# Row sums of layer 0 on column tiles, and VectorE of layer 0 in program order

## The chip, the cores and the metric

The kernel runs on one core of a Trainium2 chip. A core has a matrix engine (TensorE, "PE" in the profile, its weight loads "PEld"), VectorE ("DVE"), ScalarE ("ACT"), GpSimd ("POOL") and the sync engine ("SP"), which here issues most DMA transfers. They run side by side and wait for each other by semaphores. SBUF is the working memory of 128 partitions, PSUM the small memory in eight banks that TensorE writes. The metric is the device time of one execution in microseconds (us): the median of several runs.

## The reference, cut to what matters

Two layers on an input of 4 images of 128 channels and 64x64 pixels, all in float32. Layer 0 is attention over the 4096 pixels of each image; layer 1 (a cumulative attention and a feed-forward part with choice of experts) follows on 128-channel tokens. The change touches layer 0.

```python
def _L0_conv_ref(x, w1, b1, a1, w2, b2, a2, wa, ba, aa):
    N, C, H, W = x.shape
    HW = H * W
    e1 = _conv1x1(x, w1, b1, a1).reshape(N, -1, HW)
    e2 = _conv1x1(x, w2, b2, a2).reshape(N, -1, HW)
    asm = _conv1x1(x, wa, ba, aa).reshape(N, C, HW)
    score = jnp.einsum('nci,ncj->nij', e1, e2)
    score = jax.nn.softmax(score, axis=2)
    out = jnp.einsum('nij,ncj->nci', score, asm)
    return out.reshape(N, C, H, W)
...
x = x + _L0_conv_ref(_gn(x), L0_conv_w1, ...)
t = _to_tokens(x)
```

`_conv1x1` is a matrix product over channels, a bias and a PReLU; e1 and e2 have 64 channels, asm 128; `_gn` normalizes groups of 4 channels over the whole image.

## The kernel before

**Tiling.** For each image `b` (4) and each block `qb` of 512 queries (8) the kernel walks over 4096 keys in 16 steps `p` of two chunks of 128 keys; an image and a block, so 16 steps, is called a spot here, numbered 0 to 31. `probs` (L1978) makes scores `sc` by four matmuls, two chunks on the lower and the upper 64 rows of the array at the same time, takes `Exp` on ScalarE into `pr` (three buffers) and adds `pr` into `acc` on VectorE, with a copy in its place at p = 0. `weigh` (L1998) multiplies `pr` with the values `am`: two accumulating `av` banks, "o" for the lower and "t" for the upper 64 keys of a chunk. A float32 matmul is two records in the profile. The scores are made two steps ahead of `weigh`, by a list `queue`.

**The end of a spot** is the code under `if p == NPR - 1` in the step loop. After the last `weigh`, and the scores of the next spot's second step:

- `collect` (L2012) copies the lower half to `o` on ScalarE, adds the upper on VectorE, and folds the two halves of `acc` into `sums`.
- `row_sums` (L2030), for the spot before (`done`), sums `sums` over its 128 partitions: four matmuls with 128 columns of `sums` as weights and a column of ones moving, into `pd` (bank tag "sm"), which is copied to `rows` and inverted to `inv`.
- For a block `k` of the next image, `project` (L1928) makes queries and keys: `pe` on TensorE, ScalarE's bias into `y`, VectorE's PReLU by `z` into `e1` and `e2`, with two transfers on SP's queue (one by way of `side`); `value` (L1953) makes values: `pa` (tag "sm"), `ya`, `za`, `am`. `normal` (L1921) makes the input `xn` of the block after.
- `finish` (L2044) transposes `o` of the spot before on TensorE into `otr` (tag "x"), and VectorE multiplies by `inv` and adds the input `xr`, into `t`. `fetch` (L2023) loads the next `xr`.

Spot 0 also makes blocks 2 to 7 of image 0, on even steps. Images 1 to 3 are prepared during the image before: their statistics (`stat`, `chain`) in its first spot (image 1: spot 1), then one block at the end of each spot, two at the end of spot 1. In image 3 the ends of spots hold layer 1's first work in place of the next image: `normals`, `tokens`, `keys` (`f_pk`, silu, product, reduction), and, at `point()`, pieces of a scan that are due (`later(n, ...)` puts a piece off by n points). `LAG` blocks on, layer 1 goes on alone.

**Order.** TensorE's order is that of the program text. For the other engines a scheduler in the framework orders the instructions when the program is built, by its own estimates, and pools of buffers (one bank for each of the tags "x", "sm", "o", "t", two of "kv") add waits. `tc.manual_schedule(engines=...)` takes an engine out of that and keeps program order.

## Time and profile before

| | us |
|---|---|
| median of 3 runs | 2310.56 (2310.31 to 2311.3) |
| the profiled execution | 2303.66, span 2301.8 |
| mean granted TensorE clock | 0.995 |
| from the first `av` (25.50) to the last spot's `pd` (1529.82) | 1504.32 |
| one step in a spot, 8 `av` and 4 `sc` records | 2.57 |
| end of a spot with one projection beyond its step (22 of them) | 3.59 |
| end of spot 1, two projections | 7.14 |
| ends of spots 25 to 29 (layer 1's keys in them); of spot 30 | 10.39 to 10.40; 11.37 |

The profiled execution is one run among others; a sum of durations is held against its own time. In a timeline a row is start, length, engine, line, operation, tile written <- tiles read, shape, and in brackets the engine's idle time before and what ended it. A row with xN is N records in a run, and its length reaches from the first start to the last end, so neighbouring rows overlap in the pipeline. The granted clock is full except in a few stretches of 3.41 us or 6.83 us at half.

### The profile page before, as it was taken

The page shows a single profiled execution, that of the slowest core. Times are in us where ns is not written, and L with a number is a line of the kernel's source. Part 1 is how long each engine was busy: PE and PEld are TensorE (multiplying, and loading weights), DVE is VectorE, ACT ScalarE, POOL GpSimd, SP SyncE. Part 2 cuts the span into 40 slices and gives each one's busy share as a digit, 9 for nine tenths or more (in the row PEclk, how much of TensorE's full clock was granted, in tenths as well). Part 3 has the DMA queues.
Part 4 walks back from the last instruction along what each step waited for, and adds up shares of the span by engine and source line. Part 5 has one row for each costly group of instructions (what it writes and reads, how often), then busy time and mean ns, then how long its engine had stood idle before and what let it go on. Part 6 is the DMA issues. An engine that isn't in the chain of part 4 may idle for free.

```text
span 2301.8 us, 43187 instructions
## 1 busy us (share of the span) xinstructions
PE 2238.5 (97%) x18352; PEld 1163.8 (51%) x18352; DVE 1447.1 (63%) x2380; ACT 1092.2 (47%) x1328; POOL 174.4 (8%) x380
## 2 busy tenths in 40 slices
PE   7999999999999999999999999999999999999997
PEld 3644444444444444444444444456556555566663
DVE  7666565655666565556555666667867777875643
ACT  2343334433333443344445554445566676565751
POOL 0000000000000000000000000011121121222311
PEclk9999999999999999999999999999999999999999
DMA  2000010000010000001000000020211211213488
GB/s 76 33 12 16 10 45 9 17 9 9 11 52 9 9 12 13 9 9 44 9 5 5 5 5 10 5 50 26 66 44 40 65 52 41 59 55 116 138 322 302
DMA packets 78555, 104.77 MB, mean 46 GB/s; under 512 B 8976, under 2 KB 44816, under 8 KB 78352
## 3 DMA queue, kind: packets, MB, share of 16 engines
q1 hardware_dynamic: 77264, 99.81, 13.9%
q8 instruction: 146, 2.39, 0.4%
q0 software_dynamic: 512, 1.05, 0.2%
q10 hardware_dynamic: 576, 1.05, 0.1%
q14 instruction: 57, 0.47, 0.1%
HBM read 78.55 MB, written 17.04 MB: 42 GB/s over the span
## 4 chain that ended last, share of the span: by engine, by line
PE 87%; DVE 6%; ACT 3%; DMA 2%; issue 1%; SPq 0%; POOL 0%; ACTq 0%; DVEq 0%; POOLq 0%
PE av L2009 37%; PE sc L1984 18%; PE f_pv L1128 9%; PE f_pk L973 8%; PE f_pt L1151 3%; PE f_po L1174 2%; PE pd L2035 1%; PE f_po L1186 1%; ACT f_e1a L980 1%; PE pa L1957 1%; DMA x<-in_x_dram 1%; PE pe L1931 1%; DVE f_e1a L981 1%; DVE f_e1a L982 1%; PE f_pl L1294 1%
## 5 line engine op out<-in xcount | busy, mean ns | idle before, releaser
L2009 PE MATMUL av<-pr,am 64*128 64x512 f32 x4096 | 977.7, 592 | 2.4 <-ACT pr L1989 2.4
L1989 ACT ACTIVATE pr<-sc 128x1024 f32<-128x1024 f32 x512 | 524.1, 1024 | 781.2 <-PE sc L1984 766.9
L1996 DVE TENSOR_TENSOR acc<-acc,pr 128x1024 f32<-128x1024 f32 x480 | 586.6, 1222 | 484.8 <-ACT pr L1989 480.5
L2009 PEld LDWEIGHTS av<-pr,am 64*128 64x128 f32 x4096 | 401.8, 187 | 472.9 <-issue 458.1
L1984 PE MATMUL sc<-e,e 64*128 64x512 f32 x2048 | 534.9, 591 | 3.3 <-DMA e<-side 3.3
L1984 PEld LDWEIGHTS sc<-e,e 64*128 64x128 f32 x2048 | 201.5, 187 | 234.7 <-issue 229.2
L1128 PE MATMUL f_pv<-f_held,f_ama 128*32 128x256 f32 x4096 | 237.5, 381 | 6.1 <-ACT f_e1a L980 5.1
L973 PE MATMUL f_pk<-f_held,f_ama 128*128 128x512 f32 x512 | 234.9, 603 | 0.0
L1133 ACT ACTIVATE f_amb<-f_pv 128x1024 f32<-128x1024 f32 x128 | 131.1, 1025 | 130.1 <-PE f_pv L1128 129.4
L981 DVE TENSOR_TENSOR f_e1a<-f_e1a,f_held 128x1024 f32<-128x1024 f32 x128 | 156.9, 1226 | 48.6 <-ACT f_e1a L980 48.3
L980 ACT ACTIVATE f_e1a<-f_pk 128x1024 f32<-128x1024 f32 x128 | 129.8, 1025 | 110.3 <-PE f_pk L973 56.1
L1128 PEld LDWEIGHTS f_pv<-f_held,f_ama 128*32 128x32 f32 x4096 | 129.2, 110 | 100.7 <-ACT f_e1a L980 11.9
L982 DVE TENSOR_REDUCE f_e1a<-f_e1a 128x8 f32<-128x1024 f32 x128 | 155.2, 1217 | 3.5
L973 PEld LDWEIGHTS f_pk<-f_held,f_ama 128*128 128x128 f32 x512 | 92.5, 190 | 108.3 <-issue 101.1
L1092 POOL COPY f_held<-f_e1a 32x32 f32<-32x32 f32 x128 | 30.7, 240 | 909.8 <-DVE f_e1a L1074 564.1
L1151 PE MATMUL f_pt<-f_amb,f_held 128*32 128x128 f32 x1920 | 83.2, 276 | 0.8 <-ACT f_amb L1133 0.8
L918 POOL MEMSET f_held<- 128x1024 f32 x1 | 1.0, 957 | 1036.6 <-DVE xn L1922 1036.6
L1151 PEld LDWEIGHTS f_pt<-f_amb,f_held 128*32 128x32 f32 x1920 | 60.0, 109 | 10.4 <-issue 5.2
L1192 DVE TENSOR_TENSOR t<-t,f_po 128x512 f32<-128x512 f32 (+1 forms) x33 | 22.1, 671 | 56.0 <-PE f_po L1186 56.0
L956 ACT ACTIVATE f_xl<-t,ln_nb,ln_rs 128x128 f32<-128x128 f32 x128 | 52.8, 491 | 0.8 <-PE pa L1957 0.8
L1275 ACT ACTIVATE f_x<-t,f_gnb,f_grs 128x128 f32<-128x128 f32 x122 | 49.7, 482 | 0.4 <-DVE f_gnb L1254 0.4
L1993 DVE COPY acc<-pr 128x1024 f32<-128x1024 f32 x32 | 22.2, 694 | 39.3 <-ACT pr L1989 39.3
(300 smaller groups left out, 1797.8 us busy)
## 6 DMA issues: line engine op xcount, KB each, us to landing
f_e2a<-f_rd SPq DMA_DIRECT2D x128, 128.0 KB, 2.9
xr<-in_xtok_dram SPq DMA_DIRECT2D x32, 256.0 KB, 3.0
f_table<-f_x SPq DMA_DIRECT2D x62, 128.0 KB, 2.0
out_dram<-t SPq DMA_DIRECT2D x14, 512.0 KB, 3.8
x<-in_x_dram SPq DMA_DIRECT2D x12, 512.0 KB, 6.4
e<-e SPq DMA_DIRECT2D x32, 128.0 KB, 2.2
f_ama<-f_rd SPq DMA_DIRECT2D x16, 256.0 KB, 3.8
f_e1b<-f_rd SPq DMA_DIRECT2D x16, 256.0 KB, 6.0
```

The costliest lines, as they stand in the source:

```text
L956: nc.scalar.activation(xl[:, c, :], t[:, b * NCH + i, :], AF.Identity, bias=ln_nb[:, b, i : i + 1], scale=ln_rs[:, b, i : i + 1],)
L973: nc.tensor.matmul(pk[:, i, :], xt_at(n)[:, bass.ts(c, P)], env.wks[:, bass.ts(i, BLK)], start=True, stop=True,)
L980: nc.scalar.activation(flat, pk.rearrange("p i x -> p (i x)"), AF.Silu)
L981: nc.vector.tensor_mul(ks, ks, env.qb)
L982: nc.vector.tensor_reduce(s[:, (n % GB) * CPB + c, :], ks, AX.X, ALU.add)
L1128: nc.tensor.matmul(pv[a * CH : (a + 1) * CH, i, :], xt_at(m)[:, bass.ts(c * NA + i, CH)], env.wvs[:, bass.ts(a, HH * C)], start=True, stop ...
L1133: nc.scalar.activation(env.amb[:, bass.ts(c, HD)], pv.rearrange("p i x -> p (i x)"), AF.Silu)
L1151: nc.tensor.matmul(env.pt[i * CH : (i + 1) * CH, :], lhs, rhs, start=i not in env.begun, stop=False, skip_group_check=True,)
L1984: nc.tensor.matmul(sc[:, u, :], e2[halves[u], p, :], e1[halves[u], cols], start=True, stop=True,)
L1989: nc.scalar.activation(pr, sc, AF.Exp)
L1996: nc.vector.tensor_add(acc, acc, pr)
L2009: nc.tensor.matmul(av, am[h, j, :], pr[h, u, :], start=(j == 0), stop=(j == NCH - 1))
```

## The change

Five parts, all in layer 0:

- **Row sums.** `row_sums` now has a 128x32 block of ones as weights and 128 columns of `sums` moving, four times, each on 32 columns of the array (so each quarter of the rows of `pd` holds 128 sums, repeated 32 times). VectorE copies the result back into `sums`, `row_turn` transposes it on TensorE into a bank of tag "t" (that of the upper `av`), and `row_divide` copies every 32nd column to `rows` and inverts.
- **Order.** VectorE keeps program order in all of layer 0. `project` and `value` are cut in five parts (`project`, `value`, `queries`, `others`, `values`), `finish` in `turn_output` and `finish`; the end of a spot is written out in that order, with `row_turn` after the first block's `value` and `row_divide` after its `queries`. The fold into `sums` becomes `fold`, at the end of it all.
- **Adding up.** `add_up` does the sum of step p after `weigh` of step p (it was with the scores, two steps ahead); at p = 0 nothing is copied, at p = 1 the first two `pr` are added.
- **Image 1's load and statistics** come later: the load at step 13 of spot 0, `stat` one step later, `normal(0)` at step 14.
- **Image 3.** The first `keys` of an end comes between `row_sums` and `row_turn`; `otr` has the tag "sm"; at the end of layer 0 `row_sums` of the last spot comes at once, with `keys(LAG, 1)` ahead of `row_turn`, and `last_turn` at the next point.

```diff
@@ -1881,6 +1881,7 @@
                 make_block_diagonal(nc, gavg, C // 32)
                 nc.vector.tensor_scalar_mul(gavg, gavg, 32.0 / C)
 
+                l0.enter_context(tc.manual_schedule(engines={mybir.EngineType.DVE}))
                 made = {}
 
                 def preparation(b):
...
@@ -1926,11 +1927,15 @@
                         xn_of[k] = xn
 
                     def project(k):
-                        cols = bass.ts(k, BLK)
                         pe = ps.tile([P, BLK], F32, tag="x", name=f"pe_{b}_{k}")
                         nc.tensor.matmul(pe, w12, xn_of[k], start=True, stop=True)
                         y = tmp.tile([P, BLK], F32, tag="y", name=f"y_{b}_{k}")
                         nc.scalar.activation(y, pe, AF.Identity, bias=b12)
+                        y_of[k] = [y]
+
+                    def queries(k):
+                        (y,) = y_of[k]
+                        cols = bass.ts(k, BLK)
...
                         nc.sync.dma_start(out=e1[R:, cols], in_=e1[:R, cols])
+                        y_of[k] = (y, z)
+
+                    def others(k):
+                        y, z = y_of.pop(k)
...
@@ -1957,9 +1966,12 @@
                             nc.tensor.matmul(
                                 pa[:, c, :], xn[:, bass.ts(c, P)], was, start=True, stop=True
                             )
+                        pa_of[k] = pa
+
+                    def values(k):
                         y = tmp.tile([P, CPB, C], F32, tag="y", name=f"ya_{b}_{k}")
                         nc.vector.tensor_tensor(
-                            y, pa, bas.unsqueeze(1).to_broadcast([P, CPB, C]), ALU.add
+                            y, pa_of.pop(k), bas.unsqueeze(1).to_broadcast([P, CPB, C]), ALU.add
                         )
                         z = tmp.tile([P, CPB, C], F32, tag="z", name=f"za_{b}_{k}", bufs=1)
                         nc.vector.tensor_scalar(
@@ -1970,7 +1982,14 @@
                             op0=ALU.max, op1=ALU.add,
                         )
 
-                    return stat, (chain0, chain1, chain2), normal, project, value
+                    def make(k):
+                        project(k)
+                        value(k)
+                        queries(k)
+                        others(k)
+                        values(k)
+
+                    return stat, (chain0, chain1, chain2), normal, (project, value, queries, others, values), make
 
                 NPR = NCH // 2
                 steps = [(b, qb, p) for b in range(B) for qb in range(NBLK) for p in range(NPR)]
@@ -1987,14 +2006,18 @@
                         )
                     pr = tmp.tile([P, 2, BLK], F32, tag="pr", name=f"pr_{b}_{qb}_{p}", bufs=3)
                     nc.scalar.activation(pr, sc, AF.Exp)
+                    return pr
+
+                def add_up(b, qb, p, pr):
                     if p == 0:
+                        acc_of[b, qb] = pr
+                    elif p == 1:
                         acc = small.tile([P, 2, BLK], F32, tag="acc", name=f"acc_{b}_{qb}")
+                        nc.vector.tensor_add(acc, acc_of[b, qb], pr)
                         acc_of[b, qb] = acc
-                        nc.vector.tensor_copy(acc, pr)
                     else:
                         acc = acc_of[b, qb]
                         nc.vector.tensor_add(acc, acc, pr)
-                    return pr
 
                 def weigh(b, qb, p, pr):
                     am = made[b][2]
@@ -2015,10 +2038,13 @@
                     o = tmp.tile([P, BLK], F32, tag="o", name=f"o_{b}_{qb}")
                     nc.scalar.copy(o, lower)
                     nc.vector.tensor_add(o, o, upper_)
+                    o_of[b, qb] = (o,)
+
+                def fold(b, qb):
                     acc = acc_of.pop((b, qb))
                     sums = tmp.tile([P, BLK], F32, tag="sums", name=f"sums_{b}_{qb}", bufs=1)
                     nc.vector.tensor_add(sums, acc[:, 0, :], acc[:, 1, :])
-                    o_of[b, qb] = (o, sums)
+                    o_of[b, qb] += (sums,)
 
                 def fetch(b, qb):
                     xr = tmp.tile([P, CPB, C], F32, tag="xr", name=f"xr_{b}_{qb}", bufs=1)
@@ -2029,63 +2055,89 @@
                     pd = ps.tile([P, BLK], F32, tag="sm", name=f"pd_{b}_{qb}")
                     for c in range(CPB):
+                        rows_ = slice(c * (P // CPB), (c + 1) * (P // CPB))
                         nc.tensor.matmul(
-                            pd[:, c : c + 1], sums[:, bass.ts(c, P)], ones, start=True, stop=True
-                        )
-                    nc.vector.tensor_copy(rows[:, at], pd[:, :CPB])
+                            pd[rows_, :P], ones.to_broadcast([P, P // CPB]), sums[:, bass.ts(c, P)],
+                            start=True, stop=True,
+                        )
+                    nc.vector.tensor_copy(sums[:, :P], pd[:, :P])
+
+                def row_turn(b, qb):
+                    o, sums, xr = o_of[b, qb]
+                    pd = ps.tile([P, BLK], F32, tag="t", name=f"pdt_{b}_{qb}")
+                    nc.tensor.transpose(pd[:, :P], sums[:, :P], ident)
+                    o_of[b, qb] += (pd,)
+
+                def row_divide(b, qb):
+                    o, sums, xr, pd = o_of[b, qb]
+                    at = bass.ts(b * NBLK + qb, CPB)
+                    nc.vector.tensor_copy(rows[:, at], pd[:, : P : P // CPB])
                     inv = tmp.tile([P, CPB], F32, tag="inv", name=f"inv_{b}_{qb}")
                     nc.vector.reciprocal(inv, rows[:, at])
                     o_of[b, qb] = (o, inv, xr)
 
-                def finish(b, qb):
-                    o, inv, xr = o_of.pop((b, qb))
-                    ptr = ps.tile([P, CPB, C], F32, tag="x", name=f"otr_{b}_{qb}")
+                def turn_output(b, qb):
+                    o, inv, xr = o_of[b, qb]
+                    tag = "x" if b + 1 < B else "sm"
+                    ptr = ps.tile([P, CPB, C], F32, tag=tag, name=f"otr_{b}_{qb}")
                     for c in range(CPB):
                         nc.tensor.transpose(ptr[:, c, :], o[:, bass.ts(c, P)], ident)
+                    o_of[b, qb] = (ptr, inv, xr)
+
+                def finish(b, qb):
+                    ptr, inv, xr = o_of.pop((b, qb))
...
-                stat, chain, normal, project, value = preparation(0)
+                stat, chain, normal, parts, make = preparation(0)
                 for k in range(NBLK):
                     stat(k)
                 for f in chain:
                     f()
                 for k in range(2):
                     normal(k)
-                    project(k)
-                    value(k)
+                project, value, queries, others, values = parts
+                project(0)
+                value(0)
+                project(1)
+                for k in range(2):
+                    queries(k)
+                    others(k)
+                    values(k)
+                    if k == 0:
+                        value(1)
+                normal(2)
                 queue = [probs(*steps[0]), probs(*steps[1])]
                 done, todo = None, []
                 env.xl_pool = lambda name: tmp.tile([P, CPB, C], F32, tag="xn", name=name)
                 for n, (b, qb, p) in enumerate(steps):
-                    weigh(b, qb, p, queue.pop(0))
+                    pr = queue.pop(0)
+                    weigh(b, qb, p, pr)
+                    add_up(b, qb, p, pr)
                     if (b, qb) == (0, 0) and p % 2 == 0 and p // 2 + 2 < NBLK:
                         k = p // 2 + 2
-                        normal(k)
-                        project(k)
-                        value(k)
-                        if k == NBLK - 1:
-                            xs_of[1] = load_x(1)
+                        make(k)
+                        if k + 1 < NBLK:
+                            normal(k + 1)
                     if b + 1 < B:
                         first = 1 if b == 0 else 0
                         if qb == first:
                             if p == 0:
                                 prep[b + 1] = preparation(b + 1)
                                 todo = list(range(NBLK))
-                            stat, chain, normal, project, value = prep[b + 1]
-                            if 1 <= p <= NBLK:
-                                stat(p - 1)
-                            elif p == NBLK + 1:
-                                chain[0]()
+                            stat, chain, normal, parts, make = prep[b + 1]
+                            if 2 <= p <= NBLK + 1:
+                                stat(p - 2)
+                                if p == NBLK + 1:
+                                    chain[0]()
                             elif p in (11, 13):
                                 chain[(p - 9) // 2]()
-                            elif p == 15:
+                            elif p == 14:
                                 normal(0)
                     if b > 0 and 2 <= qb < 6 and p % 2 == 0:
                         tile_stats(tmp, b - 1, (qb - 2) * NBLK + p // 2)
@@ -2093,46 +2145,77 @@
                         close_stats(b - 1)
                     if b == B - 1 and qb > 0 and p % 4 == 3 and p < NPR - 1:
                         point()
+                    if p == NPR - 1:
+                        collect(b, qb)
                     if n + 2 < len(steps):
                         queue.append(probs(*steps[n + 2]))
+                    if n == NPR - 3:
+                        xs_of[1] = load_x(1)
                     if p == NPR - 1:
-                        collect(b, qb)
                         if done:
                             row_sums(*done)
                         mine = []
                         if todo:
                             left = NBLK - qb
                             mine = [todo.pop(0) for _ in range(-(-len(todo) // left))]
+                        fresh = done and b < B - 1
                         for k in mine:
-                            _, _, normal, project, value = prep[b + 1]
+                            _, _, normal, (project, value, queries, others, values), _ = prep[b + 1]
                             project(k)
                             value(k)
+                            if fresh:
+                                row_turn(*done)
+                                queries(k)
+                                row_divide(*done)
+                            else:
+                                queries(k)
+                            others(k)
+                            values(k)
                             if k + 1 < NBLK:
                                 normal(k + 1)
                             elif b + 2 < B:
                                 xs_of[b + 2] = load_x(b + 2)
                             else:
                                 env.hold_weights()
+                            fresh = False
                         if b == B - 1:
                             if qb == 0:
                                 env.first_rooms()
+                            else:
+                                keys(min(qb, LAG + 1) - 1, 0)
+                            row_turn(*done)
+                            row_divide(*done)
+                            if qb == 0:
                                 normals(0)
                                 tokens(0)
                             elif qb <= LAG:
-                                for c in range(CPB):
+                                for c in range(1, CPB):
                                     keys(qb - 1, c)
                                 tokens(qb)
+                            turn_output(*done)
                             if qb < LAG:
                                 normals(qb + 1)
                             point()
+                        elif fresh:
+                            row_turn(*done)
+                            row_divide(*done)
+                        if done and b < B - 1:
+                            turn_output(*done)
                         if done:
                             finish(*done)
+                        fold(b, qb)
                         fetch(b, qb)
                         done = (b, qb)
-                later(1, lambda: row_sums(*done))
-                later(1, lambda: finish(*done))
-                keys(LAG, 0)
+
+                def last_turn():
+                    turn_output(*done)
+                    finish(*done)
+
+                later(1, last_turn)
+                row_sums(*done)
                 keys(LAG, 1)
+                row_turn(*done)
+                row_divide(*done)
                 point()
 
         def last_root():
```

More of the change, by code (lines that the diff above doesn't have):

```diff
@@ L1895, in preparation @@
                     made[b] = (e1, e2, am)
-                    xn_of = {}
+                    xn_of, y_of, pa_of = {}, {}, {}
                     def stat(k):
@@ L2031, in row_sums @@
                     o, sums, xr = o_of[b, qb]
-                    at = bass.ts(b * NBLK + qb, CPB)
                     pd = ps.tile([P, BLK], F32, tag="sm", name=f"pd_{b}_{qb}")
                     for c in range(CPB):
+                        rows_ = slice(c * (P // CPB), (c + 1) * (P // CPB))
                         nc.tensor.matmul(
-                            pd[:, c : c + 1], sums[:, bass.ts(c, P)], ones, start=True, stop=True
-                        )
-                    nc.vector.tensor_copy(rows[:, at], pd[:, :CPB])
+                            pd[rows_, :P], ones.to_broadcast([P, P // CPB]), sums[:, bass.ts(c, P)],
+                            start=True, stop=True,
+                        )
+                    nc.vector.tensor_copy(sums[:, :P], pd[:, :P])
[8 more added lines that the diff above has]
+                    nc.vector.tensor_copy(rows[:, at], pd[:, : P : P // CPB])
                     inv = tmp.tile([P, CPB], F32, tag="inv", name=f"inv_{b}_{qb}")
```

## The prediction

> **What bounds the kernel now.** I read the page's busy times and slices first, then the chain of waits, then the timeline around single ends of spots. A spot is one block of 512 queries of one image: 16 steps of `probs` and `weigh`, 32 spots in layer 0.
>
> ```profile
> PE 2238.5 (97%) x18352; PEld 1163.8 (51%) x18352; DVE 1447.1 (63%) x2380; ACT 1092.2 (47%) x1328; POOL 174.4 (8%) x380
> PE 87%; DVE 6%; ACT 3%; DMA 2%; issue 1%; SPq 0%; POOL 0%; ACTq 0%; DVEq 0%; POOLq 0%
> ```
>
> TensorE is busy 97% of the span and holds 87% of the chain that ended last; inside a spot nothing else counts (a step is 8 `av` and 4 `sc` records, 2.57 us each time). VectorE is free a third of the time. So only what TensorE does, or waits for, at the ends of spots can move the time. One such end, in the timeline (start, length, engine, line):
>
> ```profile
> 174.55 1.02 PE L1984 MATMUL sc<-e,e 64*128 64x512 f32 x4
> 175.37 0.69 DVE L2017 TENSOR_TENSOR o<-o,av 128x512 f32<-128x512 f32 x1 [0.54 <-ACT o L2016]
> 175.51 1.05 PE L2035 MATMUL pd<-ones,sums 128*128 128x1 f32 x8
> 176.42 1.10 PE L1931 MATMUL pe<-xn,w 128*128 128x512 f32 x2
> 177.51 1.13 PE L1957 MATMUL pa<-was,xn 128*128 128x128 f32 x8
> 177.57 0.69 ACT L1933 ACTIVATE y<-pe,b 128x512 f32<-128x512 f32 x1 [0.92 <-PE pe L1931]
> 178.47 0.60 PE L2047 MATMUL otr<-ident,o 128*128 128x128 f32 x4
> 178.60 0.48 DVE L1935 TENSOR_SCALAR z<-y,a 128x512 f32<-128x512 f32 x1
> 179.00 1.99 PE L2009 MATMUL av<-pr,am 64*128 64x512 f32 x8
> 179.60 0.67 DVE L1938 SCALAR_TENSOR_TENSOR e<-y,z 64x512 f32<-64x512 f32 x1
> 180.30 0.42 DVE L1947 SCALAR_TENSOR_TENSOR side<-y,z 64x256 f32<-64x256 f32 x1
> ```
>
> TensorE runs from `sc` to the next `av` without a gap: 3.59 us beyond the four `sc` (174.55 + 0.86 to 179.00). 22 ends look like this one (spots 2 to 23).
>
> **The 22 ends: what TensorE saves.** `pd` takes 0.91 us now (175.51 to 176.42). Afterwards its 8 records run four at a time on column tiles. The nearest row is `f_pt` (L1151), also 128x32 weights with 128 columns moving: 32 records in 1.08 us, so 0.135 for a round of four, 0.27 for two rounds. `f_ltr` to `f_pt` and back (1801.39 to 1801.59, 1804.77 to 1804.97, starts of the last matmul of one kind and the first of the other) are each about 0.1 more than a plain step, and I put 0.09 on `pd`: 0.36, a saving of 0.55. `pa` now starts 1.09 after `pe` (176.42 to 177.51), as it waits for the bank `sm` until `rows` is read at 177.36; two records of 0.43 and the latency make it 0.95, and the new copy of `pd` is done by then: 0.14 saved. `pdt` is one more transpose, 0.11 (an `otr` is 178.47 to 179.00 for four, 0.13). Net about -0.6 of TensorE work.
>
> The page "TensorEngine Tiling (Array Packing)" of the Trainium skill, section Key Properties, says that changing the tiling mode drains TensorE. The rows agree, with about 0.1 us for each change; were `pd` to cost its 0.27 alone, the sum for 22 ends would be 2 us lower.
>
> **What the same ends lose.** `pdt` lies in the bank of `av`'s upper half, so the first upper `av` now waits until VectorE's `rows` copy (L2076) has read it. VectorE runs in program order, and that copy stands behind `z` and `e1`, and `z` waits for ScalarE's `y`. So: `pe` starts 175.51 + 0.36 = 175.87; `y` starts 1.15 later as now (176.42 to 177.57), 177.02, and ends 0.69 later, 177.71; `z` 177.75; `e1` 0.51 later, 178.27; the copy 0.70 later (`e` to `side`, 179.60 to 180.30), 178.97; it takes 0.15 (the row of `rows`); `av` follows 0.05 behind an operation of VectorE. The upper `av` starts at 179.18, against 179.00 now, although TensorE would have been free at 178.4. The lower half can start early, but that brings nothing, as this row of the end of the first spot shows, where the upper `av` had to wait for `o`:
>
> ```profile
> 83.91 0.69 DVE L2017 TENSOR_TENSOR o<-o,av 128x512 f32<-128x512 f32 x1 [0.54 <-ACT o L2016]
> 83.95 2.25 PE L2009 MATMUL av<-pr,am 64*128 64x512 f32 x7
> 84.65 0.72 PEld L2009 LDWEIGHTS av<-pr,am 64*128 64x128 f32 x5 [0.43 <-DVE o L2017]
> ```
>
> There the lower half led by 0.7 us and the step was still as long as from the upper's start. I take +0.18 for each of 22 ends, **+4.0**. The bounds: -0.6 each where the copy isn't late (-13.2), +0.5 each (+10.8) where `z` comes as long after `y` as now (0.34, from 178.26 to 178.60, behind an add that the new order puts later). I take the value between because each of its steps has a row of its own. Queued behind that upper `av` are the rest of the step and the next `sc`, and so `Exp` on ScalarE; nothing else waits for it.
>
> **The end of the first spot.** Four key blocks of image 0 are still made during spot 0:
>
> ```profile
> 68.44 1.58 PE L1984 MATMUL sc<-e,e 64*128 64x512 f32 x4 [2.11 <-DMA e<-side]
> 69.76 3.23 PE L2009 MATMUL av<-pr,am 64*128 64x512 f32 x8
> ```
>
> `sc` waits 2.1 us for the transfer of `side`, which is late because VectorE did the statistics of image 1 (L1899, up to 64.14, themselves waiting for the 2 MB load of `x`) ahead of it; afterwards `av` takes 3.23 us for what takes 1.9, since the granted clock is 0.5 from 68.98 for 3.41 us, which costs 1.7. The change puts the statistics after step 2 of spot 1 and the load at step 13: 2.1 + 1.7 + 0.4 of small waits, **-4.2** (-2.5 if `side`, queued on SP behind the four x transfers of 6.4 us, is late again). The work of the start moves `gavg` and three VectorE operations: `sc` 21.9 instead of 23.2, **-1.3**.
>
> **The end with two projections** (image 0, spot 1):
>
> ```profile
> 130.03 1.02 PE L1931 MATMUL pe<-xn,w 128*128 128x512 f32 x2
> 133.97 0.69 DVE L1968 SCALAR_TENSOR_TENSOR am<-ya,za 128x512 f32<-128x512 f32 x1
> 134.11 1.99 PE L2009 MATMUL av<-pr,am 64*128 64x512 f32 x8
> ```
>
> The second `pe` starts at 130.03 because the scheduler had put its `xn` early. In program order `xn` 1 follows `am` 0, whose VectorE chain (copy, z, e, rows, inv, side, e, ya, za, am, each by its row here) ends near 134.1. Then `pe`, `y`'s 0.69, `pa`, `otr` follow: `av` at about 136.6, +2.5, with TensorE idle some 4.6 us in between. In this trace a wait of 2.1 us was followed by 3.41 us at half clock, so I add 1.7: **+4.2** (0 to +4.5).
>
> "TensorE: Matmul & The Clock Gate", section What's actually happening, says that the clock falls to half after an idle window of about 3.4 us. The row above has it fall after 2.1 us. By either the two-projection end and the tail below would fall.
>
> **Waits inside spots.** The statistics that the scheduler bunched delay the adds: the 15 steps of spot 6 take 39.07 us, of spot 14 40.27, and spots 9 and 17, where `close_stats` takes ScalarE's tables, 39.55 each, against 38.73 elsewhere. That is 3.5 us in all. Program order spreads the statistics and the data of `close_stats` are ready, but its table loads stay; I take **-2.8** (0 to -3.5).
>
> **Image 3, ends 25 to 30.** There `otr` waits for the bank `x`, ScalarE's copy of `f_ama`:
>
> ```profile
> PE otr L2047 <- ACT f_ama L966: 6.9, 6, 1.2
> ```
>
> The change takes `sm` instead, so `av` can follow about 1.8 us sooner (1.2, and 0.6 of `pd`). But VectorE now does the keys' reductions (1.22 each), four `t` (1.13) and the fold before the add of step 0, and `Exp` of step 3 has to wait for that add to give up its `pr` buffer: I get 0.95 to 1.4 us back as a stall at the fourth `av`. Left: **-2.6** for six (-6 to +3).
>
> **The tail.** Now
>
> ```profile
> 1529.82 0.95 PE L2035 MATMUL pd<-ones,sums 128*128 128x1 f32 x8
> 1531.10 2.33 DVE L981 TENSOR_TENSOR f_e1a<-f_e1a,f_held 128x1024 f32<-128x1024 f32 x2
> 1531.19 3.66 PE L1128 MATMUL f_pv<-f_held,f_ama 128*32 128x256 f32 x64
> ```
>
> `sums` of the last spot is made at 1526.32, before the keys' products. In program order the fold comes behind the product and reduction of keys 6 (1.16 and 1.17, after ScalarE's table load 1.28 and silu 1.02), `rows` and four `t`: near 1532.9, and everything of TensorE in the tail stands behind that `pd`: `f_pv` starts near 1535.8, +4.6, with about 5 us idle. With half of a slow stretch: **+5.5** (0 to +6.3).
>
> **Costed at nothing:** 32 copies of `acc` go (L1993, 22.2 us), 32 small `pd` copies come (at most the 0.69 of a 512-column one, at least the 0.15 of `rows`). VectorE is idle half of each step; without that cover they would be worth up to 22 us. Adding sums one step later only holds a `pr` buffer longer (3 buffers; `Exp` has 0.1 to 0.6 us left after the ends by my count). The `xr` transfer (3.0 us) is used a spot later. `xs` loads of images 2 and 3 stay.
>
> **The sum:** +4.0 - 4.2 - 1.3 + 4.2 - 2.8 - 2.6 + 5.5 = +2.8 us. The profiled execution (2303.66 us, span 2301.8) becomes about 2306.5; it ran 6.9 below the median of the runs, 2310.56, from which I forecast 2313.4. 0.2% is 4.6 us, about what can be told from no change.
>
> **Rivals.**
> 1. *The rows copy is not late.* If ScalarE and VectorE get through `y`, `z`, `e1` 0.8 us sooner than by rows taken from a busy time, TensorE's -0.6 stands: -13.2 in place of +4.0, sum -14.4, 2296. For it: VectorE has less to do at that point than before. Against: `y` needs both records of `pe`, whatever else is free.
> 2. *VectorE in order becomes the bound, slower.* After an end it has the rest of `queries`, `others`, `values`, `xn`, four `t`, the fold, then the first add, near 185.3; then `Exp` of step 3 ends near 186.5 for an `av` at 187.0. From 0.5 us more it stalls every end: another 0.5 makes +11, 2324. For it: 63% busy on average, and nearly full there. Against: the slack found by rows.
> 3. *The four tiles don't overlap* and `pd` stays near 0.9: then `y` and the copy are 0.55 later still, +12, 2325. Against: the `f_pt` rows.
>
> **Chances.** The forecast's case 58% (its own range 2307 to 2320: 6 faster, 30 within 0.2%, 22 slower), rival 1 25%, rival 2 13%, rival 3 4%. So faster 31%, same 30%, slower 39%. Range 2296 to 2322: it takes in rival 1 and most of rival 2.
>
> **What would show it.** Right: `av` at such ends waiting for L2076 with the lower half started first, `pd` near 0.36; no wait for `side` at the end of spot 0; a gap of 4 to 5 us ahead of the second `pe` and ahead of the last `pd`, each with a slow stretch. Wrong: ends shorter than 3.3 us, or a wait of `av` for `Exp` in the fourth step. The forecast fails first at the 22 ends, where 0.1 us is 2.2 us of time.

## The result and the profile after

The changed kernel takes 2321.06 us (median of 6 runs, 2319.99 to 2321.45), the kernel before 2310.11 (6 runs, 2304.44 to 2311.30): a ratio of 1.0059, 95% interval 1.0049 to 1.0069. It is slower, clear of noise, where +2.8 us, no change, was forecast. The profiled execution took 2321.45 us with a span of 2319.4, 17.6 more than the span before; the profiled execution before (2303.66) lies below these six, so this difference is larger than that of the medians, 11.

```profile
PE 2241.4 (97%) x18384; PEld 1234.3 (53%) x18384; DVE 1454.0 (63%) x2380; ACT 1091.8 (47%) x1328; POOL 173.7 (7%) x380
PE 86%; DVE 7%; ACT 3%; DMA 2%; issue 1%; SPq 0%; DVEq 0%; ACTq 0%
```

The busy times and the chain's shares by engine hardly tell the two kernels apart. TensorE's waits do (engine, what it waits for: us in total, times, longest):

```profile
PE av L2032 <- ACT pr L2008: 15.5, 11, 6.4
PE pd L2061 <- DVE sums L2046: 5.2, 1, 5.2
PE pe L1931 <- DVE xn L1923: 5.0, 2, 4.6
```

The first was 2.4 us in four waits before. The other two don't appear in the list of the kernel before at all. To see where they lie, the starts of the first `av` of each spot are taken from both traces and subtracted (us):

| place | before | after | difference | forecast |
|---|---|---|---|---|
| to the first `av` | 25.50 | 24.26 | -1.2 | -1.3 |
| spot 0 | 58.45 | 56.28 | -2.2 | -4.2 |
| spot 1 and its end with two projections | 50.16 | 54.74 | +4.6 | +4.2 |
| spots 2 to 23, their 22 ends | 993.30 | 992.20 | -1.1 | +4.0 and -2.8 |
| spot 24 and its end | 44.21 | 44.99 | +0.8 | 0 |
| spots 25 to 30 and their ends | 312.80 | 309.27 | -3.5 | -2.6 |
| spot 31, to its last `av` | 38.77 | 50.09 | +11.3 | 0 |
| last `av` to the first `f_pv` | 8.01 | 14.64 | +6.6 | +5.5 |
| rest of layer 1 | 770.61 | 772.96 | +2.4 | 0 |

One place was not in the forecast at all, and it is the largest: spot 31. Its timeline (start, length, engine, line):

```profile
1498.35 9.56 SPq L1108 DMA_DIRECT2D f_e2a<-f_rd  x7
1505.41 1.23 DVE L1122 TENSOR_TENSOR f_e2a<-f_e2a 128x1024 f32<-128x1024 f32 x1 [10.00 <-DMA f_e2a<-f_rd]
1506.56 3.88 DVE L2020 TENSOR_TENSOR acc<-acc,pr 128x1024 f32<-128x1024 f32 x3
1507.87 1.02 ACT L2008 ACTIVATE pr<-sc 128x1024 f32<-128x1024 f32 x1 [9.40 <-DVE acc L2020]
1508.94 3.78 PE L2032 MATMUL av<-pr,am 64*128 64x512 f32 x8 [6.40 <-ACT pr L2008]
```

`weigh_rows(0)`, one product of layer 1, stands in VectorE's program order at step 3 of the last spot, right behind the issue of the transfers that it reads. VectorE waits 10.00 us for them, with three adds queued behind it; each add frees a `pr` buffer that `Exp` needs, and `av` needs `Exp`. So most of the transfers' time lands on TensorE. Before, the scheduler had put two more adds ahead of the same product, which then waited 5.45 us; the three `pr` buffers covered that, and TensorE did not wait:

```profile
1496.99 1.66 DVE L1996 TENSOR_TENSOR acc<-acc,pr 128x1024 f32<-128x1024 f32 x1 [0.59 <-ACT pr L1989]
1499.56 1.27 DVE L1996 TENSOR_TENSOR acc<-acc,pr 128x1024 f32<-128x1024 f32 x1 [0.92 <-ACT pr L1989]
1506.28 1.22 DVE L1122 TENSOR_TENSOR f_e2a<-f_e2a 128x1024 f32<-128x1024 f32 x1 [5.45 <-DMA f_e2a<-f_rd]
```

The wait costs a second time. The windows around it (window, length, busy us and records of PE, PEld, DVE, ACT, POOL, granted clock, DMA share, GB/s):

```profile
1503.00:1507.00 4.00, 0.00 (x0) 0.00 (x0) 1.59 (x2) 0.00 (x0) 0.01 (x1) 0.73 0.14 34
1507.00:1510.00 3.00, 1.06 (x4) 0.55 (x6) 2.79 (x3) 1.83 (x2) 0.00 (x0) 0.50 0.49 138
```

The clock is at half from 1504.81 to 1515.05, and the eight `av` of 1508.94 take 3.78 us instead of 1.88.

An end of a spot with one projection, to be read against the one of the forecast:

```profile
222.01 0.43 PE L2061 MATMUL pd<-sums,ones 128*32 128x128 f32 x8
222.37 1.13 PE L1931 MATMUL pe<-xn,w 128*128 128x512 f32 x2
223.53 0.69 ACT L1933 ACTIVATE y<-pe,b 128x512 f32<-128x512 f32 x1 [0.39 <-PE pe L1931]
224.25 0.48 DVE L1940 TENSOR_SCALAR z<-y,a 128x512 f32<-128x512 f32 x1 [1.46 <-ACT y L1933]
224.77 0.68 DVE L1943 SCALAR_TENSOR_TENSOR e<-y,z 64x512 f32<-64x512 f32 x1
224.86 1.98 PE L2032 MATMUL av<-pr,am 64*128 64x512 f32 x6
225.38 0.15 DVE L2076 COPY rows<-pdt 128x4 f32<-128x4 f32 x1
225.58 0.72 PEld L2032 LDWEIGHTS av<-pr,am 64*128 64x128 f32 x5 [0.43 <-DVE rows L2076]
```

`pd` to `pe` is 0.36 us, as forecast. The lower `av` starts at 224.86, the upper at 225.58, released by the rows copy. A spot takes 44.97 us, against 44.90 before: the column tiles' saving is given back in that wait.

The end of spot 1 and the end of layer 0:

```profile
130.05 0.54 DVE L1923 TENSOR_SCALAR xn<-x,gst,std 128x512 f32<-128x512 f32 x1
130.73 2.05 PE L1931 MATMUL pe<-xn,w 128*128 128x512 f32 x2 [4.60 <-DVE xn L1923]
...
1540.95 0.68 DVE L2046 TENSOR_TENSOR sums<-acc 128x512 f32<-128x512 f32 x1
1541.68 0.66 PE L2061 MATMUL pd<-sums,ones 128*32 128x128 f32 x8 [5.18 <-DVE sums L2046]
```

Both waits are where the forecast put them, and each has a stretch at half clock, of 6.83 us (from 129.24 and from 1538.94).

### The profile page after: what moved, and what is told of

Same layout as the page of the kernel before. It is cut to its first block, busy times and chain, and to the rows that moved or that the text cites. A ratio compares the mean times of both kernels' runs of the same rounds, so it can differ in the third digit from the quotient of the medians.

```text
span 2319.4 us, 43141 instructions
## 1 busy us (share of the span) xinstructions
PE 2241.4 (97%) x18384; PEld 1234.3 (53%) x18384; DVE 1454.0 (63%) x2380; ACT 1091.8 (47%) x1328; POOL 173.7 (7%) x380
## 4 chain that ended last, share of the span: by engine, by line
PE 86%; DVE 7%; ACT 3%; DMA 2%; issue 1%; SPq 0%; DVEq 0%; ACTq 0%
PE av L2032 37%; PE sc L2003 18%; PE f_pv L1128 9%; PE f_pk L973 8%; PE f_pt L1151 3%; PE f_po L1174 2%; DVE f_e1a L981 2%; DVE f_e1a L982 1%; PE pe L1931 1%; PE f_po L1186 1%; PE pa L1966 1%; ACT f_e1a L980 1%; PE f_pl L1294 1%; ACT pr L2008 1%; PE f_ph L1735 1%
## 5 line engine op out<-in xcount | busy, mean ns | idle before, releaser
L2032 PE MATMUL av<-pr,am 64*128 64x512 f32 x4096 | 1105.4, 593 | 15.5 <-ACT pr L2008 15.5
L2020 DVE TENSOR_TENSOR acc<-acc,pr 128x1024 f32<-128x1024 f32 x448 | 548.4, 1224 | 417.5 <-ACT pr L2008 409.8
L2032 PEld LDWEIGHTS av<-pr,am 64*128 64x128 f32 x4096 | 489.5, 187 | 443.3 <-issue 356.9
L2003 PE MATMUL sc<-e,e 64*128 64x512 f32 x2048 | 659.7, 592 | 1.3 <-DMA e<-side 1.3
L2003 PEld LDWEIGHTS sc<-e,e 64*128 64x128 f32 x2048 | 264.3, 187 | 205.6 <-issue 183.6
L2040 DVE TENSOR_TENSOR o<-o,av 128x512 f32<-128x512 f32 x32 | 22.0, 689 | 71.9 <-ACT o L2039 69.8
```

The source lines that it names most:

```text
L2003: nc.tensor.matmul(sc[:, u, :], e2[halves[u], p, :], e1[halves[u], cols], start=True, stop=True,)
L2020: nc.vector.tensor_add(acc, acc, pr)
L2032: nc.tensor.matmul(av, am[h, j, :], pr[h, u, :], start=(j == 0), stop=(j == NCH - 1))
```

## The experiments

Single runs are read by place, in their traces, where 0.1 us at one end can be seen; whole times scatter by some us. The kernel before took 2301.70 to 2311.30 us in all its runs.

**The product put off.** This asks whether the stall in spot 31 comes from `weigh_rows(0)`.

```diff
-                weigh_rows(0)
+                later(2, lambda: weigh_rows(0))
```

> One product of layer 1 (L1122, the first weights) is put off by two points, from step 3 to step 11 of the last spot, and nothing else. Theory 1 (VectorE in program order holds every later add while that product waits for its transfer, 10.0 us in the trace of the changed kernel, and so Exp and av): steps 6, 7 and 8 of spot 31, 9.14, 5.28 and 2.99 us there, go back to 2.57 each, the last av starts 9.7 us sooner, and the span is near 2309.7. Rival 2 (the stall comes from the half-speed clock and late transfers around it, and the product is only in the same place): the steps stay above 4 us and the span within 2 us of 2319.4.

Measured: span 2308.36 us, 11.05 less. Spot 31 to its last `av` takes 40.40 instead of 50.09, 9.7 less; steps 6 to 8 are back at 2.57.

```profile
1502.26 1.88 PE L2032 MATMUL av<-pr,am 64*128 64x512 f32 x8
1504.83 1.88 PE L2032 MATMUL av<-pr,am 64*128 64x512 f32 x8
1507.41 1.88 PE L2032 MATMUL av<-pr,am 64*128 64x512 f32 x8
```

The product alone is worth the 9.7 us, and the slow stretch in spot 31 goes with it. Theory 1 holds. The 1.6 us that spot 31 still has over the kernel before are steps 2 and 3, which another run explains.

**The last fold sooner.** It goes right behind `collect`, and its `sums` into the buffer of `z`.

```diff
+                        if (b, qb) == last_spot:
+                            fold(b, qb)
...
-                        fold(b, qb)
+                        if (b, qb) != last_spot:
+                            fold(b, qb)
```

> Only the last spot's fold is moved, from the end of VectorE's list to the place right after o is collected (its sums lie in the buffer of z, which is free by then). Theory 1 (the last pd waits for a fold that stands behind two operations of the keys, rows and four t): from the pd of 1533.62 to the first f_pv, 12.83 us in the changed kernel and 6.20 in the kernel before, it takes 6.5 to 7.5; the span falls by 5.3 to 6.3, with the slow stretch there gone. Rival 2 (ScalarE's table load and silu set that place): under 2 us.

Measured: from the last `av` to `f_pv` 13.72 us against 14.64, only 0.9 less; the second `pd` comes 7.46 us behind the first instead of 8.06. That is the size of rival 2. The rows:

```profile
1534.72 1.02 ACT L980 ACTIVATE f_e1a<-f_pk 128x1024 f32<-128x1024 f32 x1 [0.39 <-PE f_pk L973]
1535.78 1.23 DVE L981 TENSOR_TENSOR f_e1a<-f_e1a,f_held 128x1024 f32<-128x1024 f32 x1 [1.22 <-ACT f_e1a L980]
1538.63 1.13 DVE L2094 SCALAR_TENSOR_TENSOR t<-otr,inv,xr 128x128 f32<-128x128 f32 x4
1539.81 0.65 PE L2063 MATMUL pd<-sums,ones 128*32 128x128 f32 x8 [4.43 <-DVE t L2094]
```

The fold is done at 1534.35 here, and `pd` waits for `t` all the same. `pd` is in the bank "sm", and the change also put image 3's `otr` there, so the bank is held until `t` is written, behind the keys' product and reduction. Two waits lay on top of each other; the profile names the later one alone. ScalarE's table load does not set the place, as silu waits 0.39 us more for `f_pk` after it; but silu itself, 1.02 us, lies in the chain that `t` waits for, so rival 2 is half right. In the run with all moves, which puts the keys behind `t`, this `pd` no longer waits.

**xn sooner.** `normal(k + 1)` goes from behind `values(k)` to right behind `value(k)`.

```diff
                             value(k)
+                            if k + 1 < NBLK:
+                                normal(k + 1)
                             if fresh:
                                 row_turn(*done)
```

> Only xn of the block after is moved, at all ends with a projection, from behind the values to the place right after the copy of pd, where VectorE is idle for 1.46 us. Theory 1 (at the end of spot 1 the second pe waits 4.6 us for xn): that end goes from 11.72 us to about 7, the span falls by 4.6. At the other 22 ends the rows copy decides, so a spot stays at 44.97 us. Rival 2 (the first add after an end, and by it Exp of step 3, decides there, as xn's 0.54 us lies ahead of it): spots 2 to 23 come down to 44.5 or less, another -9 us.

Measured: spot 1 with its end 50.19 us instead of 54.74, 4.55 less; the end itself 7.17. The spots 3 to 7 stay at 44.97.

```profile
124.55 0.54 DVE L1923 TENSOR_SCALAR xn<-x,gst,std 128x512 f32<-128x512 f32 x1
126.17 1.07 PE L1931 MATMUL pe<-xn,w 128*128 128x512 f32 x2
129.24 1.13 PE L1966 MATMUL pa<-was,xn 128*128 128x128 f32 x8 [2.01 <-DVE ya L1973]
```

The second `pe` no longer waits. The second `pa` still does, 2.01 us until `ya` has read the bank "sm", with a stretch of 3.41 us at half clock behind it, so spot 2 takes 45.71 us instead of 44.62. At the plain ends the steps 2 and 3 are free of stalls now, but the spot is not shorter: the rows copy sets it, as theory 1 has it.

**The old row sums in the new order.** Nothing waits for a rows copy, `pd` is four matmuls of one column again, its rows are copied at once and nothing is transposed.

```diff
-                            pd[rows_, :P], ones.to_broadcast([P, P // CPB]), sums[:, bass.ts(c, P)],
-                            start=True, stop=True,
+                            pd[:, c : c + 1], sums[:, bass.ts(c, P)], ones, start=True, stop=True
...
-                nc.vector.tensor_copy(sums[:, :P], pd[:, :P])
+                nc.vector.tensor_copy(rows[:, at], pd[:, :CPB])
```

> The row sums alone go back to those of the kernel before (four matmuls of one column, no transpose), the order of VectorE and all else stay as changed. Theory 1 (the ends are set by the wait of the upper av for the rows copy behind z and e1, 0.72 us after the lower av): without that wait the upper av starts when TensorE gets there, 0.45 us later than the lower one does now, so 0.27 sooner than the upper; a spot takes 44.7 us instead of 44.97, 5 to 6 us less over 22 ends, and the lower and upper av start together. Rival 2 (the column tiles bring their 0.45 us and the wait is hidden by the lower half's lead): a spot takes 45.4, 10 us more.

Measured: a plain spot 44.84 us, 0.13 less than changed; spots with layer 1's statistics (10 to 12, 18 to 20) 45.23, 0.26 more, and 13 and 21, which have them too, 45.85, 0.27 more; all 22 together +0.75. The lower and upper `av` start together, as theory 1 says, but the gain is half of what it says in plain spots and a loss in the others, where step 2 takes 2.92. A second limit lies close by, seen there first. As the change stands, its column tiles bring next to nothing.

**Rows first.** `row_divide` goes ahead of `queries`.

```diff
                                 row_turn(*done)
-                                queries(k)
                                 row_divide(*done)
+                                queries(k)
```

> Only the rows copy and the reciprocal are moved ahead of z and e1 on VectorE, at the 22 ends with one projection and at that of spot 1. Theory 1 (two limits lie close together: the upper av behind the rows copy, and Exp of step 3 behind the first add after the end): the upper av starts 0.7 us sooner, with the lower one, but z, e1 and all behind them end 0.5 us later, so the fourth av waits for Exp; a spot takes 44.9 to 45.4 us against 44.97, and the end is shorter while the steps 2 and 3 are longer. Rival 2 (the rows copy is the only limit): 44.3, 15 us less over 22 ends.

```profile
224.83 0.16 DVE L2076 COPY rows<-pdt 128x4 f32<-128x4 f32 x1 [1.73 <-PE pdt L2070]
225.16 1.99 PE L2032 MATMUL av<-pr,am 64*128 64x512 f32 x8
231.05 1.22 DVE L2016 TENSOR_TENSOR acc<-pr,pr 128x1024 f32<-128x1024 f32 x1
232.38 1.02 ACT L2008 ACTIVATE pr<-sc 128x1024 f32<-128x1024 f32 x1 [3.30 <-DVE acc L2016]
```

Measured: the ends take 2.95 us (spots 13 and 21: 3.05), TensorE's own time, 0.64 less than the 3.59 before; both halves of `av` start together. But step 2 takes 3.04 and step 3 2.68, and a plain spot 44.82 to 44.83 (45.22 with the statistics), 0.7 us less over all 22. The first add of the spot ends at 232.3, `Exp` of step 3 waits 3.30 us for it (an idle time that includes its normal wait) and `av` for `Exp`. The second limit is named: theory 1.

**Adds first.** The four `t`, the fold and the load of `xr` of an end go behind the first add of the next spot.

```diff
                     add_up(b, qb, p, pr)
+                    if p == 1 and rest_of:
+                        close(*rest_of.pop())
...
-                        if done:
-                            finish(*done)
-                        fold(b, qb)
-                        fetch(b, qb)
+                        if n + 1 < len(steps):
+                            rest_of.append((done, (b, qb)))
+                        else:
+                            close(done, (b, qb))
                         done = (b, qb)
```

`close` is the four lines taken out, for the spot before and this one.

> Only the four t, the fold and the load of xr of every end are moved behind the first add of the next spot on VectorE, 1.8 us of work. Theory 1: at the 22 ends the rows copy still decides and a spot stays at 44.97, with the steps 2 and 3 back at 2.57 to 2.68 for the lower half's lead; in image 3, where the first add is late by 1.5 us, step 2 goes from 4.08 back to 2.57, 9 us less from spot 25 to 30. Rival 2 (the first add decides at all ends): 44.3 in the spots 2 to 23 too.

Measured: plain spots 44.97 as expected, with no stall at steps 2 and 3. Spots 25 to 30 take 301.54 instead of 309.27, 7.7 less (9 expected); step 2 of spots 26 to 28 goes from 4.08 to 2.57. Theory 1; spot 31 is 2.4 less too, the part that the run with the product put off had left (and its other stalls differ).

**Rows and adds first, together.** Both edits.

> Both moves together. Theory 1 (two limits): only together do they bring TensorE's saving, a spot comes to 44.3 us (44.97 - 0.7), 15 us less from spot 2 to 23, beside the 9 us of image 3; the span is near 2295. Rival 2 (TensorE's switches of tiling and the transpose cost as much as the column tiles save): a spot stays at 44.8 or more.

```profile
223.62 0.16 DVE L2076 COPY rows<-pdt 128x4 f32<-128x4 f32 x1 [1.73 <-PE pdt L2070]
223.95 1.99 PE L2032 MATMUL av<-pr,am 64*128 64x512 f32 x8
228.20 1.22 DVE L2016 TENSOR_TENSOR acc<-pr,pr 128x1024 f32<-128x1024 f32 x1
```

Measured: a spot 44.25 us, spots 2 to 23 977.08 instead of 992.20, 15.1 less, span 2289.84. The one edit alone brings 0.7 us over these spots, the other 0.2, both 15.1: two limits, either of which hides what the other one costs. The first add ends at 229.4, 5.5 us after the `av`; with the rows first alone it was 7.1 (232.3 after 225.16).

**All moves.** The five edits, and the last spot's end in another order, to clear the bank "sm":

```diff
+                            elif qb < NBLK - 1:
                                 keys(min(qb, LAG + 1) - 1, 0)
...
                             turn_output(*done)
+                            if qb == NBLK - 1:
+                                finish(*done)
+                                keys(min(qb, LAG + 1) - 1, 0)
```

> All moves at once: the product of layer 1 later, the last fold sooner, xn sooner, rows first, adds first, and at the end of the last spot the first keys behind t of the spot before, so that the last pd doesn't wait for the bank sm, which otr holds until t is written (in the run with the sooner fold it waited 4.43 us for t). Theory 1: the parts add up, as they lie at different places: spot 1 50.2 us, spots 2 to 23 22 x 44.3 + 4, image 3 300 to 303, spot 31 38.8, from the last av to the first f_pv 8 to 9; the span is near 2275, 1.1 to 1.3% under the kernel before. Rival 2 (a new wait takes the place of each): 2290 or more.

Measured: median 2281.17 us (4 runs, 2276.80 to 2282.58), ratio to the kernel before 0.9886, interval 0.9863 to 0.9908; span 2277.93. Spot 1 50.26, spots 2 to 23 976.75, 25 to 30 301.54, 31 38.77: the parts add up. Two miss: the tail takes 11.08 from the last `av` to `f_pv`, not 8 to 9, and spot 0 takes 59.05, 2.8 more than changed, with a wait of 2.42 for `side` and the slow stretch behind it. None of the moves touches spot 0, and the runs above wait 1.27 to 1.77 us there. So the transfer of `side` at the end of spot 0 was still near its limit, which the next run takes up.

**SP in program order.** Alone, in the changed kernel.

```diff
-                l0.enter_context(tc.manual_schedule(engines={mybir.EngineType.DVE}))
+                l0.enter_context(tc.manual_schedule(engines={mybir.EngineType.DVE, mybir.EngineType.SP}))
```

> The changed kernel, and only SP's queue is put in program order too within layer 0. Theory 1 (image 1's load stands later in the text, but the scheduler still puts its four transfers of 512 KB on SP's queue ahead of the last e and side of spot 0, 62.27 against 66.90 us, so that side lands late): the thirteenth step of spot 0 goes from 4.16 us to 2.57 and spot 0 from 56.28 to 54.7; all other places stay within 0.5 us. Rival 2 (the transfer of side is slow in itself): the step stays above 4 us.

SP's queue at this place, first in the changed kernel, then in this run:

```profile
62.27 2.70 SPq L1860 DMA_DIRECT2D x<-in_x_dram  x4
66.90 0.54 SPq L1960 DMA_DIRECT2D e<-side  x1
```

```profile
66.61 0.55 SPq L1960 DMA_DIRECT2D e<-side  x1
67.21 2.02 SPq L1860 DMA_DIRECT2D x<-in_x_dram  x4
```

Measured: spot 0 54.69 instead of 56.28; all its late steps are 2.57. Theory 1: the load was moved in the text alone. The scheduler, which still orders SP, put its four transfers ahead of `side` as soon as the last `xn` had read the old `x`.

**All moves, SP in program order too.**

> All moves at once as before, and SP's queue in program order. Theory 1: spot 0 goes from 59.05 us there to 54.7, the rest stays; the span is near 2273.5 and the ratio to the kernel before near 0.986. Rival 2 (transfers in program order make some other reader wait): no gain over the run without it, 2278.

Measured: median 2276.55 us (4 runs, 2275.49 to 2277.92), ratio 0.9871, interval 0.9852 to 0.9890; span 2273.63, spot 0 54.69. This version beats both kernels. What is left at the tail:

```profile
1496.23 0.33 PE L2072 MATMUL pdt<-ident,sums 128*128 128x128 f32 x1 [1.84 <-DVE sums L2067]
1498.64 0.43 PE L2063 MATMUL pd<-sums,ones 128*32 128x128 f32 x8
1502.54 0.33 PE L2072 MATMUL pdt<-ident,sums 128*128 128x128 f32 x1 [1.56 <-DVE sums L2067]
```

The two `pdt` wait for VectorE's copy of `pd`, 3.4 us in sum: the new row sums have a way through VectorE that the old ones didn't have, and here no other matmuls are left to fill it.

**The same with the old row sums.** What are the column tiles worth once nothing waits?

> All moves and SP in program order, but the row sums of the kernel before: what the column tiles and the transpose are worth once nothing waits for VectorE. Theory 1 (pd costs 0.36 instead of 0.92, the transpose 0.11 more): 44.25 + 0.45 = 44.7 us for a spot, 10 us more over 22 ends, and 0.43 more at each end of image 3, as in the first run with the old sums. Rival 2 (column tiles cost as much in switches as they save): 44.3.

Measured: a spot 44.78 us against 44.25, spots 2 to 23 988.55 against 977.97, 10.6 more; spots 25 to 30 304.10 against 301.54, 0.43 each end. Theory 1 to 0.1 us a spot.

**The new row sums alone**, in the kernel before, VectorE left to the scheduler.

```diff
                 def finish(b, qb):
+                    row_turn(b, qb)
                     o, inv, xr = o_of.pop((b, qb))
```

`row_sums` and `row_turn` as in the change, with the division in `row_turn`.

> The kernel before with nothing but the new row sums (column tiles, the copy, the transpose in the bank of the upper av, placed at the head of finish); VectorE stays with the scheduler. Theory 1 (it's the place of the rows copy in VectorE's order that decides, since the upper av waits for it): the scheduler puts that copy behind z, the fold, e, side, e and ya, so by their rows the upper av starts some 2.5 us later than in the kernel before, a spot takes 47.2 to 47.5 us, 50 us more in all. Rival 2 (the tiles alone bring their 0.45): 44.4, 10 us less.

```profile
564.07 1.12 PE L2009 MATMUL av<-pr,am 64*128 64x512 f32 x2
566.61 0.15 DVE L2047 COPY rows<-pdt 128x4 f32<-128x4 f32 x1
566.91 2.83 PE L2009 MATMUL av<-pr,am 64*128 64x512 f32 x5 [1.72 <-DVE rows L2047]
```

Measured: a plain spot 47.05 us (48.6 to 48.8 where the wait brings a slow stretch, which it does at nine of the 22 ends), spots 2 to 23 1052.82, 59.5 more than before. The lower `av` starts at 564.07, the upper 2.8 us later: theory 1. The whole is twice what was expected, though: the span is 2401.70, 99.9 more and not 50. The spots 25 to 30, which the expectation left out, take 347.14 instead of 312.80; TensorE waits 3.09 us for the rows copy at five of these ends, each time with a slow stretch of 6.83 us. The order of VectorE is what makes the new row sums bearable at all.

## Why the prediction was wrong

It had no case for the largest part of what made the kernel slower. The step that failed is in its first part: "inside a spot nothing else counts" and "So only what TensorE does, or waits for, at the ends of spots can move the time." That was read from the trace of a kernel where VectorE's order was the scheduler's. The change takes that away for all of layer 0, and image 3's steps hold layer 1's scan at `point()`, with one operation that waits for a transfer. The forecast followed VectorE's new order past the ends, the two projections and the tail, not past those points: +11.3 us, shown by the run that puts off this one product (9.7 of it, with the slow stretch) and by the one with the adds first (steps 2 and 3). It is 11.3 of the 14.8 us by which the profiled executions differ more than forecast (17.6 and 2.8). Without it the sum of the places above would be 6.3 us, of which 2.4 lie in the rest of layer 1, where nothing was changed. This rest takes 770.05 to 775.26 us in the edited runs, so the 2.4 are within its scatter.

That the median, 2321.06 us, still lies in the stated range of 2296 to 2322 is luck: the upper part of that range stood for rival 2, a stall at every end, and the spots 2 to 23 with their 22 ends took 1.1 us less than before.

Point by point:

- **The 22 ends.** The mechanism was right, and so was `pd` at 0.36: the upper `av` waits for a rows copy behind `y`, `z` and `e1`, and the saving is lost. The size was +0.07 us a spot instead of +0.18; `e` to the rows copy takes 0.61, not the 0.70 taken from `e` to `side`. That is +1.5 over 22 ends; the rest of the -1.1 there, -2.6, is mostly the waits inside spots, forecast as -2.8. In `pd`'s 0.36 two errors cancel: a round of four `f_pt` records takes 0.11 us by their starts, not 0.135 (the 1.08 us hold the run-out of the last), and the change of tiling takes more than 0.09 (`pe` starts 0.22 behind the second round).
- **Rival 2 was half true.** The first add after an end is a limit of its own: with the rows first it alone sets 44.82 us in plain spots and 45.22 in those with statistics, against 44.97. The forecast's sign for it, a wait in the fourth step, does show in the changed kernel: step 2 takes 2.80 us, 3.19 in the spots with statistics. But with the adds first it is 2.57 again and the spot still 44.97, so this limit does not decide there, and does at once when the rows copy is moved.
- **Rival 1**, no late rows copy, did not happen, and its price of -13 us was about right for the version in which both limits are gone: 44.25 us a spot against 44.90 in the kernel before, 14.3 us over 22.
- **Spot 0**: -2.2 instead of -4.2, just short of the bound of -2.5. The forecast named the reason, `side` behind the load on SP's queue, but took from the text that the load had moved. With SP in program order it is -3.8.
- **Two projections**: +4.6 for +4.2, just above the bound of +4.5. The wait was forecast as 4.6 us and is 4.60; the slow stretch lasts 6.83 us and not 3.41.
- **Image 3**: -3.5 for -2.6, with a stall of 1.5 us at step 2, where 0.95 to 1.4 was forecast. Spot 24, where `otr` now waits 0.7 us for `f_ama`, was left out: +0.8.
- **The tail**: +6.6 for +5.5, above the bound of +6.3. The wait for the fold was right, 5.18 us for about 5. The slow stretch was counted by half, as 0.9; 4.1 us of it lie behind the wait, by half of which it cost an estimated 2.0. That the bank "sm" makes nearly the same wait was not seen, and was the next bound.

By the page "TensorE: Matmul & The Clock Gate" of the Trainium skill, section What's actually happening, an idle window of about 3.4 us brings half clock. The traces here have it after shorter ones: in the changed kernel after about 3.1 us (TensorE ends `pdt` at 126.13, the clock falls at 129.24), in the kernel before after a wait of 2.11, with the new row sums alone after one of 1.72 (the clock falls at 566.98). Nor does a wait's length settle it: a wait of 2.26 us of the second `pa` is followed by half clock with all moves and SP in program order (from 128.69), and by none with all moves alone.

## What to carry to other kernels

Where an engine is taken out of a scheduler's hands, follow it from the first to the last instruction of the region, and look for each operation that waits for a transfer: in program order all that stands behind it waits too, and a few buffers cover only a few us (here 5.45 us, with two adds ahead of the wait, but not 10.00). A place that costs nothing in one trace can be held by two limits at once, so test a suspected wait together with the next one; here two edits that brought 0.7 and 0.2 us alone brought 15.1 together. Moving a load in the text moves it in the queue only if that queue keeps the text's order.

## What was not expected of the hardware

- The stretches at half clock that end within the trace last 3.41, 6.83 or 10.24 us. They can begin before the wait is over, in the changed kernel at 129.24, 1.5 us ahead of the `pe` that ends it, or just after, in the kernel before at 68.98, 0.5 us behind the start of `sc`. If half of the slow time behind a wait is lost, the waits of 4.4 to 6.4 us in these runs cost 1.5 to 3.4 us more; this is an estimate.
- The two halves of the array do not stay together. In the changed kernel the lower `av` start 0.72 us before the upper ones at an end, and a score matmul starts (226.68) while one of the eight `av` of the step is still to start (226.97), though the text has all eight ahead of it. With the adds first the lead is held for a spot's length (ends of 3.67 us by the first `av`, against 2.95 where both halves start together), and it is no gain: a spot takes 44.97 us with the lead kept or lost.
